# Spreading two weight rows through DRAM and reordering the first group's preparation in a two-layer graph attention kernel

## The chip, the cores and the metric

One core of one Trainium2 chip. The time is the device time of the whole program in microseconds, taken over several runs; one further execution is profiled. Engines are named as the profile names them: PE is TensorE (matrix products and transposes; PEld its weight loads), DVE is VectorE, ACT is ScalarE, POOL is GpSimd, SP is SyncE, which here only issues DMAs. ScalarE issues DMAs too (ACTq).

## The reference

`x` is 64 graphs of 256 nodes with 512 features, `adj` 64 matrices of 256x256 with zeros and ones, all float32. Two layers follow one another:

```python
# layer 0: one head, additive scores
fp = x @ fc_w.T + fc_b
q = fp @ q_w.T + q_b                     # one number for each node
k = fp @ k_w.T + k_b
s = q + k.T + (1 - adj) * -1e9
s = where(s >= 0, s, 0.01 * s)
x = softmax(s) @ fp + x
# layer 1: eight heads, scores with a bias by nodes and log(adj + 1e-9)
Q, K, V = x @ W_q + b_q, x @ W_k + b_k, x @ W_v + b_v
s = Q @ K.T / 8 + (x @ w_g[:512])[:, None] + (x @ w_g[512:])[None, :] + b_g + log(adj + 1e-9)
x = softmax(s) @ V + x
```

In layer 0 the chain x, fp, q can be joined: q is x times one row of 512 numbers, `q_w @ fc_w`, plus a constant, and k likewise.

## The kernel before

The 64 graphs go in 32 groups of two (T = 4 tiles of 128 nodes). A `Group` object has a method for each small step, and `step` writes out by hand, for a window of groups, the order in which the steps of layer 0 of one group, the projections and the attention of layer 1 of another are issued. The schedule is manual: each engine works through its instructions in the order in which the code issues them, and only waits where data or buffers are missing. The products of 512x512 weights are done with seven instead of eight block products (Strassen's scheme in Winograd's form), for which VectorE forms sums of weight blocks once (`blocks_of_weights`, four half-sums of 128x512 for each of wk, wq, wv and fc; the lines L335 to L338) and sums of token blocks for every group.

The change touches only the beginning: the setup and what the first group needs, since it has no older group beside it (`features_first`, in place of the later groups' `mix` and `pf` products). In the order of the code before:

- The weight fc_w is loaded by ScalarE's queue, x, adj (four DMAs), wq, wk, wv and the row wgc_row by SP's queue. `columns` (L249) turns short rows of parameters into columns. `rows_of_x` (L261) multiplies q_w and k_w by fc_w, which gives a 2x512 tile on two partitions (`rows_qk_sb`, copied out of PSUM at L266).
- `spread_rows` (L273, L277) copies each of the two rows to all 128 partitions: a product with a broadcast column of the identity on TensorE into a PSUM bank, and a copy by ScalarE into `wq_row` and `wk_row`. It stands after the first of four tiles of transposes of x (L705), whose results VectorE copies into xT (L706).
- fc_w is transposed (L152; ScalarE copies fcT out, L153). VectorE forms `dot_q` and `dot_k` for the four tiles (L519: multiplies x by the row and sums up), with the constant kqc of k between them (L291).
- `product(t)` (L718) is the feature product of one tile; ScalarE copies it (L722). `queries` (L581) turns q into a row on all partitions by way of TensorE.
- `adjt` (L562) turns adj by 32x32 blocks on VectorE and forms the mask (L564). `weights` (L604, L608 on VectorE, the exponential at L609 on ScalarE) gives layer 0's softmax weights e, `sums` (L658) their sums on TensorE, and `recip_of_sums` (L667, L668) their reciprocals.
- `constants_of_projections` (L301, TensorE, 16 products of 128x256) and its `add` (L313, L317, L318) bring fc_b's part into the biases of layer 1's projections, which lie in the columns `cols_1`.
- In the last loop each tile t of x1 is formed: a product with e (L750), two of the half-sums of wv and fc, then x1 = product * reciprocal + x (L756) on VectorE; then x1 is turned on TensorE (`x1t`, L811, copied by ScalarE at L816).

After that `step` goes on with `pq.p1` (L412), the first block product of layer 1's queries, `pk.p1` and `pv.p1`, the sums of token blocks `xsum` (L375), `keys` (L519, with wgc_row) and the load of the next group's x, which waits for `keys`. Later groups send their q through DRAM to spread it (`spread`, L591 and L593): a write of the 128x4 tile and a broadcast read to 128 partitions.

The PSUM pool `ps` has four banks, taken in turn; one of them holds the constant `pk` until L291 has read it.

Of the kernel before, what the change touches and what calls it, by code (L numbers as in the profile page):

```python
# [10 lines left out]
F32 = mybir.dt.float32  # L11
# [6 lines left out]
P = 128  # L18
# [7 lines left out]
def kernel(  # L26
# [64 lines left out]
    nc = tc.nc  # L91
    NB, N, D = x.shape
# [53 lines left out]
    def transposed_weights(w, pool, psum, copy):  # L146

        t = pool.tile([P, NC, D], F32, tag="fcT", name="fcT")
        for hc in range(NC):
            pt = psum.tile([P, 512], F32, tag="bank", name=f"pfc_{hc}")  # L150
            for oc in range(NC):
                nc.tensor.transpose(pt[:, ts(oc, P)], w[:, oc, ts(hc, P)], ident)  # L152
            copy(t[:, hc, :], pt)  # L153
        return t

    wk_row = const.tile([P, D], F32, tag="wk_row", name="wk_row")
    wq_row = const.tile([P, D], F32, tag="wq_row", name="wq_row")
    kqc = const.tile([P, 1], F32, tag="kqc", name="kqc")

    NR = 4  # L160
# [3 lines left out]
    def fast():  # L164
        main = ExitStack()
        with main:
# [12 lines left out]
            def bank(name):  # L179
                return ps.tile([P, 512], F32, tag="bank", name=name)  # L180
# [87 lines left out]

            def spread_rows(rows):

                for n, dst in enumerate((wq_row, wk_row)):
                    pt = bank(f"row_{n}")
                    nc.tensor.matmul(  # L273
                        pt, lhsT=ident[0:2, n : n + 1].to_broadcast([2, P]), rhs=rows,
                        start=True, stop=True,
                    )
                    nc.scalar.copy(dst, pt)  # L277

            def constant():

# [248 lines left out]
            class Group:  # L529
# [167 lines left out]
                def features_first(self):  # L697

                    g = self.g
                    xT = one.tile([P, NC, TOK], F32, tag="qT", name=f"xT_{g}")  # L700
                    fp = v_all
                    for t in range(T):
                        pt = bank(f"xTp_{g}_{t}")
                        for c in range(NC):
                            nc.tensor.transpose(pt[:, ts(c, P)], self.x[:, t, ts(c, P)], ident)  # L705
                        nc.vector.tensor_copy(  # L706
                            xT[:, :, ts(t, P)], pt.rearrange("p (c n) -> p c n", c=NC)
                        )
                        if t == 0:
                            spread_rows(rows_qk)  # L710
                    fcT = transposed_weights(fc_nat, wts, ps, nc.scalar.copy)
                    for t in range(T):
                        self.dot_q(t)

                    def product(t):
                        pp = bank(f"fp_{g}_{t}")
                        for c in range(NC):
                            nc.tensor.matmul(  # L718
                                pp, lhsT=xT[:, c, ts(t, P)], rhs=fcT[:, c, :],
                                start=(c == 0), stop=(c == NC - 1),  # L720
                            )
                        nc.scalar.copy(fp[:, t, :], pp)  # L722

                    product(0)
                    self.queries()
                    k_constant()
                    for t in range(T):
                        self.dot_k(t)
                    self.adjt(True)
                    product(1)  # L730
                    self.weights(0)
                    self.weights(1)
                    self.add_eps()
                    product(2)
                    add_constants = constants_of_projections()
                    for name, wt in (("k", wk_sb), ("q", wq_sb)):
                        for issue in blocks_of_weights(wt, name):
                            issue()
                    self.sums()
                    columns(rows_1, cols_1, "cols_1")  # L740
                    product(3)
                    add_constants()
                    self.recip_of_sums()
                    self.begin()
                    sums = blocks_of_weights(wv_sb, "v") + blocks_of_weights(fcT, "fc")
                    for t in range(T):
                        gr, ic = divmod(t, TPG)
                        po = bank(f"x1p_{g}_{t}")
                        for j in range(TPG):
                            nc.tensor.matmul(  # L750
                                po, lhsT=self.e0[:, j, gr, ts(ic, P)], rhs=fp[:, gr * TPG + j, :],
                                start=(j == 0), stop=(j == TPG - 1),
                            )
                        for issue in sums[2 * t : 2 * t + 2]:
                            issue()
                        nc.vector.scalar_tensor_tensor(  # L756
                            self.x[:, t, :], po, recip0[:, g, t : t + 1], self.x[:, t, :],
                            ALU.mult, ALU.add,
                        )
                        if t > 0:  # L760
                            self.x1t(t - 1)
                    self.x1t(T - 1)


                def begin(self):
# [341 lines left out]
            def step(d, a, f, n, check):  # L1107


                def of(group):  # L1110
                    def issue(pieces):
                        for piece in pieces.split():
                            name, *args = piece.split(":")
                            if group is None:
                                continue
                            target = group
                            if "." in name:
                                part, name = name.split(".")
                                target = getattr(group, part)
                            getattr(target, name)(*map(int, args))  # L1120
                    return issue

                D, A, F, X = of(d), of(a), of(f), of(n)
                f.older = d
                X("load_adj")
                if a is not None:
                    attention_and_layer_0(D, A, F, X)
                else:
                    f.features_first()
                    F("pq.p1 pq.keep_1 copy:0 pk.p1 pk.keep_1 pv.p1 pv.keep_1")  # L1130
                F("xsum:0 xsum:1 xsum:2 pq.p6")
                A("factor:3:0 factor:3:1 both:3")
                F("keys:2 keys:3 keys:0 keys:1")
                X("load_x")
                F("pq.p7 pq.p2 pq.sum_00 xsum:3")
                check()
                F("pq.p5 pk.p6 pq.sum_11 pq.p3")
                A("divide:0")
                X("dot_q:0 dot_q:1 dot_q:2 dot_q:3 spread")
                F("pq.p4 pq.sum_10 copy:1 copy:2")  # L1140
                A("complete:0 store:0 parts:2")
                if n is None:
                    A("parts:3")
                F("pk.p7 pk.p5 pk.sum_11 residual:0")
                X("adjt")
                F("pk.p2 pk.sum_00")
                X("dot_k:0 dot_k:1")
                F("pk.p3 pk.p4 pk.sum_10")
                X("dot_k:2 dot_k:3")
                F("turn_residual:0")  # L1150
                if n is None:
                    A("attend:1 totals_1 ratios:1 turn:1 divide:1 complete:1 store:1")
                    F("residual:1 turn_residual:1")

                    F("pv.p2 scores:0 pv.p6 pv.sum_00 factor:0:0 factor:0:1 scores:1 both:0 pv.p7")
                    F("factor:1:0 factor:1:1 both:1 scores:2 pv.p5 sums_1:0 scores:3 pv.sum_11")
                    F("ratios_t:0 ratios_r:0 factor:2:0 factor:2:1 pv.p3 pv.p4 factor:3:0 pv.sum_10")
                    F("factor:3:1 attend:0 finish:0 sums_of_e:1 attend:1")
                    F("ratios_t:1 ratios_r:1 finish:1")
                    check_ranges()()  # L1160
                    return
                X("mask add_eps")
                F("pv.p2 pv.p6")
                X("weights:0")
                F("pv.p7 pv.p5")
                X("weights:1")
                F("pv.sum_00")
                A("parts:3")

            with tc.manual_schedule(engines=ENGINES):  # L1170
                f = Group(0)
# [4 lines left out]
                    nc.tensor.matmul(warm[:, 0:P], lhsT=ident, rhs=ident, start=True, stop=True)  # L1176
                columns(rows_0, cols_0, "cols_0")
                rows_qk = rows_of_x()
                k_constant = constant()
                d, a, a_w = None, None, {}  # L1180
                for g in range(NG):
# [224 lines left out]
```

## Time and profile before

| What | Value |
|---|---|
| median of 4 runs | 2311.5 us (2310.65 to 2312.56) |
| profiled execution, its own time | 2312.43 us |
| its span | 2310.6 us |
| mean granted TensorE clock | 0.998 |
| idle time of TensorE in the span | 15.5 us |
| start of the first block product of layer 1 | 45.13 us |
| DMA traffic | 163.84 MB, mean 71 GB/s |
| adj, 128 KB, from issue to landing | 3.6 us (median) |

The span is that of the profiled execution's instructions; its own time is 1.8 us longer. Times inside the profile count from the start of the span. A row of the costliest groups gives line, engine, operation and tiles, and then the busy time, the mean of one instruction and the idle time ahead of it with what ended it. The chain of waits is followed back from the last instruction and says on which engine the time that matters was spent; in its order of time each row is a start, a length on the chain and what ran. A row of the timeline is a start, a length, engine, line, operation and tiles. The granted clock is the share of TensorE's full clock.

### The profile page before, as it was taken

What the parts mean: (1) busy time and instruction counts of PE and PEld (TensorE: products, weight loads), DVE (VectorE), ACT (ScalarE), POOL (GpSimd) and SP (SyncE); (2) the same over time, 40 slices, a digit from 0 to 9 for tenths busy, and PEclk for the clock granted to TensorE, in tenths of its full rate; (3) what the DMA queues carried; (4) which work ended last, traced back from release to release, by engine and by line L of the source; (5) the groups of instructions that cost most, each with busy time, mean ns of one, the idle gap of its engine ahead of it and who ended that gap; (6) DMA issues with size and microseconds to landing.
All of it is one profiled execution on the core that took longest, in us unless ns stands there. A gap on an engine that the chain in (4) does not pass through costs nothing.

```text
span 2310.6 us, 33613 instructions
## 1 busy us (share of the span) xinstructions
PE 2295.1 (99%) x12618; PEld 1902.9 (82%) x12618; DVE 2124.3 (92%) x3180; ACT 1072.2 (46%) x1865; POOL 121.9 (5%) x120
## 2 busy tenths in 40 slices
PE   9999999999999999999999999999999999999997
PEld 5888888888888888888888888888888888888885
DVE  6899999999999999999999999999999999999997
ACT  3544445444445444444444444444544445444443
POOL 0000000000000000000000000000000000000000
PEclk9999999999999999999999999999999999999999
DMA  4122323223323233232233232332223323323312
GB/s 133 42 65 74 78 74 69 65 65 81 84 64 69 60 78 78 74 66 64 69 78 80 63 72 63 81 78 74 61 63 74 78 73 70 64 64 80 84 47 38
DMA packets 517264, 163.84 MB, mean 71 GB/s; under 512 B 415188, under 2 KB 478696, under 8 KB 517096
## 3 DMA queue, kind: packets, MB, share of 16 engines
q1 hardware_dynamic: 514440, 160.32, 29.1%
q8 instruction: 102, 1.67, 0.3%
q10 hardware_dynamic: 2656, 1.31, 0.2%
q14 instruction: 66, 0.54, 0.1%
HBM read 95.43 MB, written 66.12 MB: 70 GB/s over the span
## 4 chain that ended last, share of the span: by engine, by line
PE 98%; DVE 1%; DMA 0%; ACT 0%; issue 0%; ACTq 0%; DVEq 0%
PE pv L412 17%; PE pq L412 17%; PE pf L412 16%; PE pk L412 16%; PE sc L859 11%; PE oT L899 10%; PE y L689 9%; PE fp L718 1%; DMA fc_nat<-in_L_gnn_fc_w_dram 0%; PE rc L637 0%; PE xTp L705 0%; DVE osb L1034 0%; PE tot L927 0%; DVE osb L1040 0%; DVE osb L1033 0%; DVE x L756 0%
## 5 line engine op out<-in xcount | busy, mean ns | idle before, releaser
L873 ACT ACTIVATE e<-sc,c 128x1024 f32<-128x1024 f32 x254 | 269.0, 1110 | 79.1 <-PE sc L859 77.6
L879 DVE TENSOR_TENSOR e<-e,am 128x1024 f32<-128x1024 f32 x254 | 297.8, 1213 | 0.4 <-ACT e L873 0.4
L859 PE MATMUL sc<-qT,kT 64*128 64x256 f32 x2048 | 255.8, 389 | 0.4 <-ACT e L873 0.4
L899 PE MATMUL oT<-e,v 128*64 128x256 f32 x2032 | 233.4, 382 | 0.0
L859 PEld LDWEIGHTS sc<-qT,kT 64*128 64x128 f32 x2048 | 187.2, 186 | 52.8 <-issue 32.8
L495 POOL TENSOR_TENSOR pf_s<-pf_s,x 128x512 f32<-128x512 f32 x93 | 118.4, 1273 | 2107.9 <-ACT pf_s L494 2040.5
L689 PE MATMUL y<-e,x 128*128 128x256 f32 x992 | 225.6, 380 | 0.0
L899 PEld LDWEIGHTS oT<-e,v 128*64 128x64 f32 x2032 | 140.2, 137 | 85.4 <-DVE x L501 10.3
L689 PEld LDWEIGHTS y<-e,x 128*128 128x128 f32 x992 | 186.2, 190 | 24.0
L432 ACT ACTIVATE pq_s<-pq,cols 128x256 f32<-128x256 f32 x192 | 80.5, 470 | 249.1 <-PE pq L412 249.1
L494 ACT ACTIVATE pf_s<-pf,recip 128x256 f32<-128x256 f32 x186 | 77.9, 470 | 197.6 <-PE pf L412 197.6
L917 DVE TENSOR_REDUCE part<-est 128x32 f32<-128x1024 f32 x124 | 151.3, 1220 | 4.3
L916 DVE STREAM_TRANSPOSE est<-es 128x1024 f32<-128x1024 f32 x124 | 152.3, 1229 | 0.0
L886 DVE TENSOR_TENSOR es<-e,e 128x1024 f32<-128x1024 f32 x126 | 149.3, 1206 | 1.1
L695 ACT COPY yT<-y 128x512 f32<-128x512 f32 x124 | 72.6, 585 | 131.6 <-PE y L689 130.9
L429 ACT COPY pk_s<-pk 128x512 f32<-128x512 f32 x96 | 56.3, 586 | 165.7 <-PE pk L412 159.0
L906 ACT COPY oTs<-oT 128x512 f32<-128x512 f32 x128 | 75.0, 586 | 117.3 <-PE oT L899 96.5
L412 PE MATMUL pk<-t1b,wk 128*128 128x256 f32 x512 | 121.1, 379 | 0.4 <-DVE kT L443 0.4
L412 PE MATMUL pv<-wv,t1b_c 128*128 128x256 f32 x512 | 121.1, 379 | 0.0
L412 PE MATMUL pv<-wv,t1b 128*128 128x256 f32 x512 | 121.1, 379 | 0.0
L412 PE MATMUL pq<-x1T,wq 128*128 128x256 f32 x512 | 121.0, 379 | 0.0
L412 PE MATMUL pk<-t1b,k_s 128*128 128x256 f32 x512 | 121.0, 379 | 0.0
(181 smaller groups left out, 4505.9 us busy)
## 6 DMA issues: line engine op xcount, KB each, us to landing
x<-in_x_dram SPq DMA_DIRECT2D x32, 1024.0 KB, 5.1
out_dram<-osb SPq DMA_DIRECT2D x254, 128.0 KB, 3.1
xd<-xt SPq DMA_DIRECT2D x124, 256.0 KB, 2.0
x1T<-xd SPq DMA_DIRECT2D x496, 64.0 KB, 2.0
adj<-in_adj_dram SPq DMA_DIRECT2D x128, 128.0 KB, 3.6
qrow<-q SPq DMA_DIRECT2D x31, 256.0 KB, 4.2
fc_nat<-in_L_gnn_fc_w_dram ACTq DMA_DIRECT2D x4, 256.0 KB, 4.9
wq<-in_L_gnn_W_q_dram SPq DMA_DIRECT2D x1, 1024.0 KB
```

Source lines behind the costliest of these rows:

```text
L412: nc.tensor.matmul(o, lhsT=lk[:, ts(m, P)] if len(lk.shape) == 2 else lk[:, m], rhs=rk, start=(start and m == 0 and k == 0), stop=(m == 1 ...
L432: nc.scalar.activation(dst[:, m], src[:, m], AF.Identity, bias=self.bias[:, 2 * o + m : 2 * o + m + 1],)
L494: nc.scalar.mul(s[:, m], src[:, m], self.recip[:, TPG * k + m : TPG * k + m + 1])
L495: nc.gpsimd.tensor_tensor(s, s, self.out(o, k), ALU.add)
L689: nc.tensor.matmul(y[:, ts(gr, N)], lhsT=self.x[:, gr * TPG + j, ts(c, P)], rhs=self.e0[:, j, gr, :], start=(gr == 0 and j == 0), stop=(gr ...
L859: nc.tensor.matmul(sc[:, par, pr, :], lhsT=self.kT[rows, 2 * hg + pr, ts(t, P)], rhs=self.qT[rows, 2 * hg + pr, ts(gr, N)], start=True, st ...
L873: nc.scalar.activation(e, sc, AF.Exp, bias=self.c[:, t : t + 1], scale=SCALE)
L879: nc.vector.tensor_tensor(ef, ef, self.am[:, jc, u // 2, :].unsqueeze(1).to_broadcast([P, 4, N]), ALU.mult,)
L886: nc.vector.tensor_tensor(self.esum[u], self.e[u, 0], self.e[u, 1], ALU.add)
L899: nc.tensor.matmul(oT[par * HD : (par + 1) * HD, pr, :], lhsT=self.v[:, gr * TPG + jc, ts(h, HD)], rhs=self.e[2 * gr + hg, jc][:, par, pr, :],
L916: nc.vector.transpose(turned, self.esum[u].rearrange("p a b i -> p (a b i)"))
L917: nc.vector.tensor_reduce(self.part[:, hg, :], turned.rearrange("p (m c) -> p m c", c=B), AX.X, ALU.add,)
```

## The change

- `spread_rows` no longer uses TensorE and PSUM. ScalarE issues a DMA that writes the 2x512 tile to DRAM (4 KB), waits for it, and issues a second DMA that reads the 1024 numbers back to each of the 128 partitions of one tile `qk_rows` (512 KB). It is called right after `rows_of_x` and `constant`, before the transposes of x.
- `adjt(True)` moves from behind `dot_k` to before `dot_q` on VectorE.
- The four feature products stand nearly in a row: `queries` comes between the second and the third, and the fourth now precedes `sums`.
- k's half-sums come directly behind `weights`; `constants_of_projections` and `columns` go behind `sums`, `recip_of_sums` behind the first x1 product, the addition of the constants behind the second. q's and v's half-sums stand in the loop over t (before: v's and fc's).
- fc's half-sums are issued in `step`, after `xsum` 0 to 2 and `pq.p6`.
- `add_eps` (ScalarE) moves behind the constants.

```diff
--- before.py
+++ after.py
@@ -153,8 +153,8 @@
             copy(t[:, hc, :], pt)
         return t
 
-    wk_row = const.tile([P, D], F32, tag="wk_row", name="wk_row")
-    wq_row = const.tile([P, D], F32, tag="wq_row", name="wq_row")
+    qk_rows = const.tile([P, 2, D], F32, tag="qk_rows", name="qk_rows")
+    wq_row, wk_row = qk_rows[:, 0], qk_rows[:, 1]
     kqc = const.tile([P, 1], F32, tag="kqc", name="kqc")
 
     NR = 4
@@ -268,13 +268,11 @@
 
             def spread_rows(rows):
 
-                for n, dst in enumerate((wq_row, wk_row)):
-                    pt = bank(f"row_{n}")
-                    nc.tensor.matmul(
-                        pt, lhsT=ident[0:2, n : n + 1].to_broadcast([2, P]), rhs=rows,
-                        start=True, stop=True,
-                    )
-                    nc.scalar.copy(dst, pt)
+                d = dram.tile([2 * D], F32, tag="qk", name="qk_rows_d")
+                nc.scalar.dma_start(d.rearrange("(n h) -> n h", n=2), rows)
+                nc.scalar.dma_start(
+                    qk_rows.rearrange("p n h -> p (n h)"), d.unsqueeze(0).to_broadcast([P, 2 * D])
+                )
 
             def constant():
 
@@ -706,9 +704,8 @@
                         nc.vector.tensor_copy(
                             xT[:, :, ts(t, P)], pt.rearrange("p (c n) -> p c n", c=NC)
                         )
-                        if t == 0:
-                            spread_rows(rows_qk)
                     fcT = transposed_weights(fc_nat, wts, ps, nc.scalar.copy)
+                    self.adjt(True)
                     for t in range(T):
                         self.dot_q(t)
 
@@ -722,27 +719,23 @@
                         nc.scalar.copy(fp[:, t, :], pp)
 
                     product(0)
-                    self.queries()
                     k_constant()
                     for t in range(T):
                         self.dot_k(t)
-                    self.adjt(True)
                     product(1)
+                    self.queries()
+                    product(2)
                     self.weights(0)
                     self.weights(1)
+                    for issue in blocks_of_weights(wk_sb, "k"):
+                        issue()
+                    product(3)
+                    self.sums()
+                    add_constants = constants_of_projections()
+                    columns(rows_1, cols_1, "cols_1")
                     self.add_eps()
-                    product(2)
-                    add_constants = constants_of_projections()
-                    for name, wt in (("k", wk_sb), ("q", wq_sb)):
-                        for issue in blocks_of_weights(wt, name):
-                            issue()
-                    self.sums()
-                    columns(rows_1, cols_1, "cols_1")
-                    product(3)
-                    add_constants()
-                    self.recip_of_sums()
                     self.begin()
-                    sums = blocks_of_weights(wv_sb, "v") + blocks_of_weights(fcT, "fc")
+                    sums = blocks_of_weights(wq_sb, "q") + blocks_of_weights(wv_sb, "v")
                     for t in range(T):
                         gr, ic = divmod(t, TPG)
                         po = bank(f"x1p_{g}_{t}")
@@ -751,6 +744,10 @@
                                 po, lhsT=self.e0[:, j, gr, ts(ic, P)], rhs=fp[:, gr * TPG + j, :],
                                 start=(j == 0), stop=(j == TPG - 1),
                             )
+                        if t == 0:
+                            self.recip_of_sums()
+                        if t == 1:
+                            add_constants()
                         for issue in sums[2 * t : 2 * t + 2]:
                             issue()
                         nc.vector.scalar_tensor_tensor(
@@ -760,6 +757,7 @@
                         if t > 0:
                             self.x1t(t - 1)
                     self.x1t(T - 1)
+                    self.later = blocks_of_weights(fcT, "fc")
 
 
                 def begin(self):
@@ -1129,6 +1127,9 @@
                     f.features_first()
                     F("pq.p1 pq.keep_1 copy:0 pk.p1 pk.keep_1 pv.p1 pv.keep_1")
                 F("xsum:0 xsum:1 xsum:2 pq.p6")
+                if a is None:
+                    for issue in f.later:
+                        issue()
                 A("factor:3:0 factor:3:1 both:3")
                 F("keys:2 keys:3 keys:0 keys:1")
                 X("load_x")
@@ -1176,6 +1177,7 @@
                     nc.tensor.matmul(warm[:, 0:P], lhsT=ident, rhs=ident, start=True, stop=True)
                 columns(rows_0, cols_0, "cols_0")
                 rows_qk = rows_of_x()
+                spread_rows(rows_qk)
                 k_constant = constant()
                 d, a, a_w = None, None, {}
                 for g in range(NG):
```

## The prediction

> **What bounds the kernel now.** I read first the totals of the page and the shares of its chain of waits, then the busy time of each engine in two stretches (0 to 11 us is the first load), then the chain in order of time for the start, and last VectorE's timeline there.
>
> ```profile
> PE 2295.1 (99%) x12618; PEld 1902.9 (82%) x12618; DVE 2124.3 (92%) x3180; ACT 1072.2 (46%) x1865; POOL 121.9 (5%) x120
> PE 98%; DVE 1%; DMA 0%; ACT 0%; issue 0%; ACTq 0%; DVEq 0%
> ```
> ```profile
> 11.00:45.30 34.30, 33.68 (x158) 18.86 (x158) 28.19 (x56) 11.90 (x23) 0.00 (x0) 0.95 0.48 131
> ```
> ```profile
> 45.30:2300.00 2254.70, 2252.79 (x12438) 1880.33 (x12437) 2091.57 (x3109) 1058.80 (x1841) 118.38 (x93) 1.00 0.29 69
> ```
>
> The columns after the stretch are its length, the busy time of PE, PEld, DVE, ACT and POOL, the granted clock, the DMA share and GB/s. From 45.3 us on TensorE stands still for 1.9 us in 2254.7. The diff takes nothing from TensorE there; it touches the first group's preparation, which ends when `pq.p1`, the first product of layer 1, starts. So the sum is one number: how far that start moves. Every later product follows it one for one, as long as nothing that the change pushes behind it becomes late.
>
> ```profile
> 11.80 1.91 PE row L273 x4
> 13.71 2.50 PE xTp L705 x12
> ...
> 18.83 3.43 PE fp L718 x8
> 22.26 0.44 PE qrow L581 x4
> 22.70 6.87 PE fp L718 x16
> 29.57 1.86 PE pc L301 x32
> 31.43 0.44 PE sm L658 x16
> ...
> 32.02 3.63 PE fp L718 x8
> ...
> 35.91 0.37 DVE cols L317 x4
> ...
> 36.46 0.09 DVE recip L668
> ...
> 43.82 0.71 DVE x L756
> ...
> 45.29 1.73 PE pq L412 x8
> ```
>
> The reader should see two stretches. Up to 35.9 us the chain lies on TensorE, almost without a gap. From 36.46 us it lies on VectorE: the reciprocals, then eight half-sums of weights of 0.6 to 0.7 us and four rows of x1 of 0.7 us with no idle time, until the last x1 at 43.82 us; 1.47 us later `pq.p1` starts. What counts is when the reciprocals start, and what VectorE has to do behind them.
>
> ```profile
> 16.85 0.68 DVE L519 CUSTOM_DVE_ANT_0 jq<-x,wq_row 128x512 f32<-128x512 f32 x1
> 23.08 1.24 DVE L562 STREAM_TRANSPOSE am<-adj 128x1024 f32<-128x1024 f32 x1
> ```
> ```profile
> qrow<-q SPq DMA_DIRECT2D x31, 256.0 KB, 4.2
> ```
>
> The dots with the rows of q and k begin at 16.85 us, and adj is turned after them.
>
> **TensorE up to the sums.** Taken out are the two products that spread the rows (1.91 us on the chain at 11.80) and two ScalarE copies (0.58 and 0.59 us, beside other work). Without them the first feature product starts at 18.83 - 1.91 = 16.9 us; the copies of xT on VectorE (0.69 us each) and the copies of fcT on ScalarE can hold it to about 18. The four products now come ahead of the sums: 3.43 + 3.44 + 0.44 (queries) + 3.43 + 3.63 = 14.4 us. TensorE could thus start the sums of e (`sm`) at 16.9 + 14.4 = 31.3 us.
>
> **The rows by way of DRAM.** The rows are in SBUF at 11.37 us (ScalarE's copy, 10.80 + 0.57). The nearest row is the same trip that each later group makes for q: its first transfer was issued at 61.81 us and the second at 63.28 us, 1.47 us later, and the second, 256 KB, lands 4.2 us after its issue. Here the second is 512 KB. The traffic of the 256 KB was spread over 2.1 us (six slices of 0.35 us), so I add 2.1 us: 11.4 + 1.5 + 6.3 = 19.2 us with the engines free. They aren't: from 13 to 25 us the DMA share is 0.94 to 1.09 in every microsecond, first with adj (small packets, about 160 GB/s), then with three weights of 1 MB. Sharing with them I estimate at 2 us more: 21.2 us. The bound above is the row of `wgc_row`, 256 KB broadcast too, which took 10.0 us behind those weights: 11.4 + 1.9 + 10.0 = 23.3 us. The bound below is 19.2 us.
>
> The Trainium skill's page "DMA: Bandwidth & Descriptors", section "Anatomy of one DMA", speaks against such a trip: each DMA pays about 2 us whatever its size, most of it the receipt of the last write, heaviest where DRAM is written. The trace has 1.47 us for the small write to DRAM, less than the page. By the page the two would take 2.0 and 2.0 + 512 KB at 436 GB/s = 3.2 us and be there at 16.6 us; the rows would then not decide and the sum would be that with adj alone, below.
>
> ScalarE waits for the first transfer with the copies of fcT behind it. The fcT transposes that feed them begin at 13.5 us at the earliest (11.80 + 1.7 for the remaining transposes at the speed of the first four), so the wait, over by 12.9 us to 13.5 us, hides in front of them. If it lasted to 16 us, the first product would lose its 1.9 us again.
>
> **Adj first.** The turning of adj and the mask take 2.1 us (23.08 to 25.16) and now precede the dots. The last adj transfer is issued at about 13.6 us and lands 3.8 us later, at 17.4 us; before, 5 us of dots covered this, now VectorE waits for it from 14.7 us (four copies of 0.72 us from 11.84). So the dots cannot start before 17.4 + 2.1 = 19.5 us. With the broadcast taking a share of the same 16 engines I put the landing 1.3 us later: 20.8 us. The dots start at J = the later of the two, 21.2 us, between 19.5 and 23.3.
>
> From the dots to the sums VectorE's rows are: dots 16.85 to 23.16 = 6.3 us, weights 25.16 to 29.05 = 3.9 us, last exponential 0.67 us; together 10.9 us. The queries on TensorE need only the first half of the dots (J + 2.9 = 24.1 us, against 16.9 + 6.9 = 23.8 us). The sums start at 21.2 + 10.9 = 32.1 us, 0.8 us behind what TensorE could.
>
> **Constants behind the sums.** From the sums to the reciprocals there are now 0.44 (sm) + 1.86 (pc) + 0.15 (columns) + 1.8 (first x1 product, a quarter of 7.2 us) + 0.3 (turn of the sums and start) = 4.55 us: 32.1 + 4.55 = 36.65 us, against 36.46. The half-sums of k are done before that (J + 10.2 + 2.9 = 34.3 us), and VectorE idles about 2 us there. Behind the reciprocals stand again eight half-sums (q and v in place of v and fc) and four x1, and in addition the constants of the columns, 0.37 + 0.16 = 0.53 us, which before lay ahead. So `pq.p1` moves by 36.65 - 36.46 + 0.53 = +0.7 us: the 1.9 us that TensorE saves are used up, because VectorE both starts the dots 4 us later and carries as much work behind the reciprocals as before.
>
> **Behind `pq.p1`.** The four half-sums of fc (2.8 us) go in front of `keys`. VectorE idles 5.1 us there before it adds qT at 55.76 us, which hides them. The load of the next x waits for `keys`: it moves from 50.71 to 53.5 us and lands 5.1 us later at 58.6 us; the dots that read it begin at 58.90 us. If that cover failed by 1 us, the next addition (62.60 us, 0.8 us of idle time ahead of it) would slip by 0.2 us. fc itself is wanted only by group 1's feature product. On SP's queue nothing is moved; adj of group 1, which waits for the turning, is issued some 3 us earlier, behind the weights. I cost all this at nothing.
>
> **The sum.** The profiled execution took 2312.43 us with a span of 2310.6 us. With +0.7 us it would take 2313.1; the median of the four runs lies 0.9 us below the profiled one, so 2311.5 + 0.7 = 2312.2 us.
>
> **The rivals.** A difference of 0.2% is 4.6 us; that is about what a measurement of this kernel can tell from no change.
>
> First: the saving passes through. If the transfers hardly disturb each other, J = 19.5 us, the sums start where TensorE allows, at 31.3 us at the latest, and the move is 31.3 + 4.55 - 36.46 + 0.53 = -0.1 us. If also the dip of the clock (granted 0.50 from 14 to 17 us, 0.82 in the next microsecond, a loss of 1.7 us) doesn't recur, J alone holds: 30.4 + 4.55 - 36.46 + 0.53 = -1.0 us, 2310.5. For it: adj has landed by 17.4 us in the trace. Against it: the saturated engines. It cannot give 4.6 us, since the 1.9 us of products and 1.7 us of clock are all there is to gain.
>
> Second, the other side: the broadcast is starved on the way to the dots. Each microsecond of J beyond 20.4 us goes to the end undiminished, as VectorE has no slack between the dots and the sums. At 23.3 us the move is +2.8 us, 2314.3. From J = 25.1 us it is over 4.6 us; if the rows had to wait until the weights' traffic ends at 25.3 us, with a microsecond for the landing, the move is +5.8 us, 2317.3. For it: `wgc_row`'s 10 us, and that both transfers stand in the fullest stretch of the trace. Against it: fc_w on ScalarE's queue and x on SP's shared the same engines at the start, both 1 MB, and finished within 1.3 us of each other, so a second queue isn't left behind.
>
> **How the numbers follow.** The forecast (-0.5 to +2 us) gets 0.63, the saving passing through 0.15, the rows late but under 4.6 us 0.10, the rows late by more 0.09; what I have not seen, 0.03. The scatter of the four runs is about 1 us to each side of the median. The range goes from the first rival's -1.0 us less 1.1 (2309.4) to the bound of `wgc_row`, +2.8 us and 1.1 (2315.4), and leaves out the starved case. Faster by over 0.2%: 0.03; slower: 0.11; within: 0.86.
>
> **What would show it.** In the profile after, the dots (jq) start near 21 us with an idle spell of some 6 us before the turning of adj, ended by a DMA; the first feature product starts near 17 us; `sm` follows the exponential, not the fourth product; the reciprocals stand near 36.7 us, with v's and q's sums and the constants behind them and no idle time; `pq.p1` starts at 46.0 us. I am wrong if the rows land after 25 us, if ScalarE's copies of fcT wait past 16 us, or if TensorE stands still after `pq.p1`.

## The result, and the profile after

| | before | after |
|---|---|---|
| median | 2311.24 us (60 runs, 2309.58 to 2312.93) | 2314.82 us (40 runs, 2313.23 to 2316.64) |
| profiled execution | 2312.43 us, span 2310.6 us | 2314.62 us, span 2312.8 us |

The ratio is 1.0015 (95% interval 1.0011 to 1.0019): the change makes the kernel 3.6 us slower (2.5 to 4.4). That is within 0.2% and inside the range, but the sum had +0.7 us. The profiled pair differs by 2.2 us.

The totals of the page and the two stretches first, with the columns as before:

```profile
PE 2293.2 (99%) x12614; PEld 1899.6 (82%) x12614; DVE 2124.1 (92%) x3180; ACT 1071.9 (46%) x1863; POOL 122.0 (5%) x120
```
```profile
11.00:45.30 34.30, 31.37 (x154) 16.10 (x153) 25.29 (x52) 10.56 (x21) 0.00 (x0) 1.00 0.55 146
45.30:2300.00 2254.70, 2252.93 (x12438) 1879.52 (x12436) 2094.05 (x3113) 1059.44 (x1841) 118.41 (x93) 1.00 0.29 69
```

The long stretch is what it was: TensorE stands still for 1.8 us in it (1.9 before), in the same 12438 instructions. In the short one TensorE has 2.3 us less work, and the clock is 1.00 where it was 0.95. Of the chain of waits after, in order of time (start, length, what ran), these pieces carry the start:

```profile
12.87 5.96 DMA adj<-in_adj_dram
18.85 1.26 DVE am L560
20.73 0.68 DVE jq L517
30.79 0.64 ACT e L607
31.47 0.43 PE sm L656 x8
33.78 1.91 PE x1p L743 x4
35.84 0.18 DVE recip L666
45.19 1.73 PE pq L410 x8
```

From 11 us on the chain no longer lies on TensorE: it waits for the load of adj, goes to VectorE, and stays there up to the exponential at 30.79 us. `pq.p1` starts at 45.19 us, 0.1 us *earlier* than before (45.29). In this pair the 2.2 us are therefore not in the first group, and not in the steady part either. The last work instruction of both kernels, VectorE's cast of the final flag, and the engine queues' waits at the end show where they are (timeline of before, then of after; then SyncE's waits from 2303 us, in us, count, longest, of before and of after):

```profile
2304.47 0.14 DVE L1101 CAST flag<-oks 1x1 int32<-1x1 f32 x1
```
```profile
2304.61 0.14 DVE L1099 CAST flag<-oks 1x1 int32<-1x1 f32 x1
```
```profile
SPq L1401 <- PEq L1401: 0.6, 2, 0.4
```
```profile
SPq L1403 <- PEq L1403: 2.6, 2, 2.4
```

The casts end 0.13 us apart. From there to the end of the span it is 5.96 us before and 8.09 us after. In this tail nothing of the result is computed: every engine reads the flag, branches past the general version of the program that the kernel keeps for other inputs, drains and meets the rest. The rows of the program's closing line (L1401, L1403) show who is late (duration in ns as least, median, most, then first and last start; before, then after):

```profile
L1401 DVEq DRAIN  x2: 10/14/17, 2309.7 to 2310.1; - x2
```
```profile
L1403 ACTq DRAIN  x2: 8/8/8, 2306.4 to 2310.4; - x2
L1403 DVEq DRAIN  x2: 17/73/129, 2310.0 to 2312.5; - x2
```

ScalarE reaches its last drain at 2310.4 us, VectorE at 2312.5 us; before, both were there at 2310.1. So the profiled pair puts nearly the whole difference (2.1 of 2.2 us) at the end of the program, 2260 us behind the change.

### The profile page after: what moved, and what is told of

Same layout as the page of the kernel before. It is cut to its first block, busy times and chain, and to the rows that moved or that the text cites. A ratio compares the mean times of both kernels' runs of the same rounds, so it can differ in the third digit from the quotient of the medians.

```text
span 2312.8 us, 33603 instructions
## 1 busy us (share of the span) xinstructions
PE 2293.2 (99%) x12614; PEld 1899.6 (82%) x12614; DVE 2124.1 (92%) x3180; ACT 1071.9 (46%) x1863; POOL 122.0 (5%) x120
## 4 chain that ended last, share of the span: by engine, by line
PE 97%; DVE 2%; DMA 1%; ACT 0%; SPq 0%; issue 0%; DVEq 0%
PE pv L410 17%; PE pq L410 17%; PE pf L410 16%; PE pk L410 16%; PE sc L857 11%; PE oT L897 10%; PE y L687 9%; DMA x<-in_x_dram 0%; DMA adj<-in_adj_dram 0%; PE rc L635 0%; DVE jk L517 0%; DVE osb L1032 0%; PE tot L925 0%; DVE osb L1038 0%; DVE osb L1031 0%
```

## The experiments

Two things had to be told apart: what the change does to the first group, and what the tail does. Two figures serve as measure in every run. The *preparation* is the start of `pq.p1` minus the start of the first transposition of x (`xTp`), both from the timeline; counted like this, the arrival of x, which puts that transposition anywhere from 9.85 to 11.46 us, drops out. The *tail* is the time from the end of the flag's cast to the end of the span. With 11 runs of a variant, an interval is about 0.09% to each side, 2 us; what is smaller rests on rows of the profiles. "Records" counts everything that VectorE executed in the trace, its waits for semaphores included.

| Kernel | median, us | ratio (95%) | preparation, us | VectorE records | tail, us |
|---|---|---|---|---|---|
| before (profiled) | 2311.24 | 1 | 33.96 (clock dip) | 3725 | 5.96 |
| before_again | 2311.67 (one) | | 33.76 (clock dip) | 3725 | 5.94 |
| before_less | 2313.57 | 1.0011 (1.0002 to 1.0020) | 32.66 | 3720 | 8.28 |
| before_pad8 | 2312.13 | 1.0004 (0.9995 to 1.0013) | 32.64 | 3733 | 6.68 |
| after (profiled) | 2314.82 | 1.0015 (1.0011 to 1.0019) | 34.25 | 3721 | 8.09 |
| after_again | 2315.08 (one) | | 34.34 | 3721 | 8.11 |
| after_pad8 | 2313.49 | 1.0008 (0.9999 to 1.0018) | 34.74 | 3729 | 6.51 |
| rows_by_te | 2315.12 | 1.0016 (1.0007 to 1.0025) | 34.22 | 3721 | 7.77 |
| dots_first | 2314.82 | 1.0016 (1.0007 to 1.0025) | 32.92 | 3723 | 8.74 |
| reorder_only_pad8 | 2313.57 | 1.0006 (0.9997 to 1.0015) | 34.21 | 3731 | 6.55 |
| dram_alone_pad8 | 2313.46 | 1.0005 (0.9996 to 1.0014) | 36.34 (clock dip) | 3733 | 6.85 |
| dots_first_pad8 | 2313.24 | 1.0007 (0.9998 to 1.0016) | 39.32 (clock dip) | 3731 | 6.53 |
| dots_first_q_pad8 | 2312.71 | 1.0004 (0.9995 to 1.0014) | 33.02 | 3731 | 6.63 |
| rows_on_sp | 2310.57 | 0.9996 (0.9987 to 1.0005) | 31.51 | 3730 | 6.78 |

The kernel before stood at 2311.51, 2311.49 and 2311.28 us beside the three sets of runs.

The two measures carry nearly everything. The stretch between them, from the start of `pq.p1` to the end of the cast, is 2259.5 to 2260.1 us in all profiles but that of dots_first_q_pad8 (2260.9). Preparation plus tail, less the 38.6 us of a before without the dip of the clock (32.65 + 5.95), gives the difference of each variant's median to the before beside it to within 0.7 us. The exceptions are dram_alone_pad8 and dots_first_pad8, where the profiled execution was the slowest of its set.

**after_pad8: eight idle instructions more on VectorE.** The theory for the tail: what counts is how many instructions VectorE executes. The change takes none of its work (3180 busy instructions in both profiles), but four of its semaphore waits.

```diff
+    extra = const.tile([P, 8], F32, tag="extra", name="extra")
+    for n in range(8):
+        nc.vector.memset(extra[:, n : n + 1], 0.0)
```

> The changed kernel with eight tiny VectorE instructions (128x1 memsets of a tile that nobody reads) ahead of everything, in VectorE's idle first 5 us. Theory: 2.1 us of the loss lie behind the work, where VectorE's last instruction waits for instruction loading because the change shortened VectorE's stream by four instructions. Then the end of the work (the flag's cast) stays where it is in the changed kernel, the tail from there to the end of the span falls from 8.1 to 6.0 us, and the time is 2314.8 - 2.1 = 2312.7 us. Rival, the whole loss lies in the first 45 us and the tail's 2 us are chance: 2314.8 us.

Measured: 2313.49 us, 1.3 us below after where 2.1 was expected, and the tail is back to 6.51 us (8.09). More instructions and less time: the tail's cost is not one of work. The preparation of this profile is half a microsecond longer (34.74 us), because here the rows land last, at 20.15 us: VectorE waits 2.96 us for them with adj already turned. The last wait of SyncE is as short as before:

```profile
SPq L1406 <- PEq L1406: 0.6, 2, 0.4
```

**before_less: fewer instructions in the kernel before.** The same theory from the other side. The edit leaves out the first of the range checks of the softmax reciprocals, that of groups 0 to 3, and touches nothing of the change.

```diff
-    if d is not None and (d.g % NR == NR - 1 or d.g == NG - NR // 2 - 1):
+    if d is not None and d.g > NR and (d.g % NR == NR - 1 or d.g == NG - NR // 2 - 1):
```

> The kernel before without the first of its range checks of the reciprocals (groups 0 to 3): at least five VectorE instructions fewer, and nothing else. Theory: VectorE's stream is then as short as in the changed kernel, its last instructions fall on the far side of the same boundary, the tail grows from 6.0 to 8.1 us and the time from 2311.2 to 2313.3 us although the kernel does less; if six fewer step past the boundary again, 2311.2 us. Rival, instruction places don't matter: 2311.2 us or a little less, tail 6.0 us.

Measured: 2313.57 us; with less work the old kernel is 2.1 us slower. VectorE executes five records fewer, and its very last one, a semaphore instruction, comes at 2311.9 us, where TensorE's is at 2310.3 (closing line, columns as above):

```profile
L1401 DVEq EVENT_SEMAPHORE  x2: 21/21/21, 2309.7 to 2311.9; - x2
```

**rows_by_te: the new order, but the rows spread by TensorE again.** It asks whether the trip through DRAM matters at all.

```diff
-                d = dram.tile([2 * D], F32, tag="qk", name="qk_rows_d")
-                ...
+                for n, dst in enumerate((wq_row, wk_row)):
+                    pt = bank(f"row_{n}")
+                    nc.tensor.matmul(
+                    ...
+                    nc.scalar.copy(dst, pt)
...
+                        if t == 0:
+                            spread_rows(rows_qk)
...
-                spread_rows(rows_qk)
```

> The changed kernel with the rows spread by TensorE as before; everything else of the change is kept. Theory, adj's landing holds the dots, not the rows: the first feature product moves 1.9 us later, adj lands some 0.7 to 1.3 us earlier for want of the broadcast (dots at 19.4 to 20.0 us in place of 20.7), the sums follow TensorE at about 31.3 us, and the first product of layer 1 starts within 0.5 us of the changed kernel's 45.0 us: 2314.8 us, or 2312.7 us if the tail is short. Rival, the trip through DRAM is what costs (the step of the prediction): the dots move 2 us or more and the time falls by over 1 us beyond the tail. Second rival, the trip brings its full 1.9 us: 1.9 us slower than the changed kernel.

Measured: 2315.12 us against 2314.82, preparation 34.22 against 34.25 us. The two products and copies that the change takes out, 1.91 us of TensorE on the old chain, are worth nothing in the new order, but not because the same wait decides in both. Here the chain lies on TensorE, as the expectation said of the sums, and VectorE waits for the row of `queries` (chain of waits, then VectorE's timeline):

```profile
17.70 6.87 PE fp L719 x16
24.57 0.44 PE qrow L581 x4
25.01 6.87 PE fp L719 x16
31.87 0.57 PE sm L658 x16
```
```profile
26.21 1.27 DVE L604 SCALAR_TENSOR_TENSOR e<-qrow,kq,e 128x256 f32<-128x256 f32 x2 [0.70 <-ACT qrow L586]
```

VectorE waits only 0.90 us for adj (4.93 in after) and begins the dots at 19.20 us, 7.8 us after the first transposition, where after takes 10.0 us. The last transfer of adj takes 3.7 us from issue to landing here and 6.0 us in after, beside the broadcast. So what the trip through DRAM saves on TensorE, it loses by holding up adj.

**dots_first: after with adj turned behind the dots again.**

```diff
                     fcT = transposed_weights(fc_nat, wts, ps, nc.scalar.copy)
-                    self.adjt(True)
                     for t in range(T):
                         self.dot_q(t)
...
                     for t in range(T):
                         self.dot_k(t)
+                    self.adjt(True)
                     product(1)
```

> The changed kernel with adj turned behind the dots again; everything else of the change is kept. Theory: the rows are there at about 16.2 us, so the dots start at 16.3 us in place of 20.7, the turning hides behind them, the sums start at about 29.5 us and layer 1's first product 1.9 us earlier than in the changed kernel, at about 43.1 us: 2312.9 us with a tail of 8 us, 2310.8 us with one of 6 us. Rival, the rows through DRAM come too late by themselves: the dots wait for them past 19 us and the gain is under 0.5 us.

In the profile it is right: the dots start at 16.93 us, the preparation is 32.92 us, 1.3 us shorter than in after. But the median stays at 2314.82 us, because the tail is 8.74 us (3723 records), and because the runs scatter over 5 us (2313.5 to 2318.4): the dots now depend on the arrival of the rows alone, which is the likely reason (the profiled execution is the fastest of them). The tail had to be taken out of the comparison, so the next kernels carry the eight instructions too.

**reorder_only_pad8: both undone, only the moved products, sums and constants left** (the edits of rows_by_te, dots_first and after_pad8 together).

> The changed order of products, constants and half-sums alone: the rows are spread by TensorE and adj is turned behind the dots, both as before, and eight tiny VectorE instructions at the start keep the end of the program clear of the boundary (tail about 6 us). Theory: the order itself costs. The first feature product starts at about 17.4 us, four products lead to sums at 31.8 us, 4.55 us more to the reciprocals, and behind them stand eight half-sums and the constants: layer 1's first product at 45.6 us, where the kernel before without a dip of the clock has 43.7 us. Time 2311.3 + 1.9 = 2313.2 us. Rival, the order is harmless and only adj ahead of the dots costs: 43.7 us and 2311.3 us.

Measured: `pq.p1` at 45.45 us, preparation 34.21 us, against 32.64 us in before_pad8. The new order costs 1.6 us by itself. Here it is TensorE again: with its two products of rows it begins the feature products at 17.41 us, `queries` now stands behind two of them in place of one (24.28 us, in before_pad8 21.07), VectorE waits for it, and the sums come behind the fourth product at 31.68 us (30.22). From VectorE's timeline:

```profile
26.07 1.26 DVE L607 SCALAR_TENSOR_TENSOR e<-qrow,kq,e 128x256 f32<-128x256 f32 x2 [1.66 <-ACT qrow L589]
```

**dram_alone_pad8: the kernel before, with the rows by way of DRAM and nothing else of the change** (the new `spread_rows`, called ahead of `constant` as in after, and the eight instructions).

> The kernel before with the rows sent through DRAM, nothing else changed but the eight tiny VectorE instructions. Theory: TensorE saves its 1.9 us but the sums of e wait for the exponentials, whose dots start no earlier than before (rows at 16.2 us or later); layer 1's first product stays within 0.5 us of 43.7 us and the time within 0.7 us of 2311.3 us. Rival, the saving passes through: 2309.4 us.

Measured: 2313.46 us, between 2311.48 and 2315.71, and so slower than expected. The profiled execution is the slowest of them: VectorE waits 5.66 us for the rows and begins the dots at 19.79 us, and the clock dips at 23.21 us. In that execution the saving does not pass through in the old order either, because the rows come late; the other runs were not profiled.

**dots_first_pad8** is dots_first with the eight instructions.

> The changed kernel with adj turned behind the dots, with eight tiny VectorE instructions at the start. Theory: the work is as in the run without them (flag at about 2303 us, first product of layer 1 at 43.3 us), and the tail falls from 8.7 to about 6.2 us: 2314.8 - 2.5 = 2312.3 us by the median. Rival, the scatter of that run had another cause than the tail: no change from 2314.8 us.

The tail came down as expected (6.53 us). The median, 2313.24 us, is 1 us above the expectation, and the profiled execution (2318.23 us) shows why the runs spread up to there: its rows landed at 21.8 us, and VectorE stood still for 8.1 us.

```profile
21.97 0.69 DVE L520 CUSTOM_DVE_ANT_0 jq<-x,qk_rows 128x512 f32<-128x512 f32 x1 [8.13 <-DMA qk_rows<-qk_rows_d]
```

**dots_first_q_pad8** is dots_first_pad8 with q's half-sums formed while VectorE waits for the sums, in place of behind the reciprocals.

```diff
                     sums = blocks_of_weights(wq_sb, "q") + blocks_of_weights(wv_sb, "v")
+                    for issue in sums[:4]:
+                        issue()
+                    sums = [lambda: None] * 2 + sums[4:] + [lambda: None] * 2
```

> The same with q's four half-sums issued ahead of the reciprocals, into VectorE's idle time, so that only v's four stand behind them (two between the second and third x1, two before the fourth... one pair ahead of x1 of tile 1 and one ahead of tile 2). Theory: behind the reciprocals VectorE then has 2.8 us less to do, the reciprocals come about 0.4 us later, TensorE becomes the limit and layer 1's first product starts at 42.6 to 43.0 us: 0.4 to 0.8 us less than with the half-sums of q behind. Rival, VectorE was not what held the x1 tiles: no change.

Measured: 2312.71 us, 0.5 us less. The profiled execution began its dots at 17.95 us, when the rows had landed, and `pq.p1` at 43.53 us, later than the 42.6 to 43.0 us expected; its preparation is 33.02 us. The step is within the noise of the runs.

**rows_on_sp: the same kernel, but SyncE issues the two DMAs of the rows, ahead of adj, the weights and wgc_row.** If the scatter of the rows comes from the transfers they share the DMA engines with, this takes it away.

```diff
-            adj_0 = load_adj(0)
...
-            wq_sb = weights(W_q, "wq", wts)
-            ...
-            wgc_row = row(w_g[D : 2 * D], "wgc_row")
...
-                nc.scalar.dma_start(d.rearrange("(n h) -> n h", n=2), rows)
-                nc.scalar.dma_start(
+                nc.sync.dma_start(d.rearrange("(n h) -> n h", n=2), rows)
+                nc.sync.dma_start(
...
                 spread_rows(rows_qk)
...
+                f.a = load_adj(0)
+                wq_sb = weights(W_q, "wq", wts)
+                ...
+                wgc_row = row(w_g[D : 2 * D], "wgc_row")
```

> The last variant (adj turned behind the dots, q's half-sums ahead of the reciprocals, eight tiny VectorE instructions) with the trip of the rows issued on SP's queue and adj and the weights issued behind it, so that nothing of size runs beside the broadcast. Theory, it is the company of adj and the weights that makes the rows late and scattered: the rows land about 3.8 us after the second issue, at 16.2 to 16.8 us, in every run; the dots start then, the sums near 29.8 us, layer 1's first product at 42.6 to 43.0 us; adj lands near 20 us, in time for its turning at 22.4. Median 2310.4 us, 0.9 us under the kernel before, with a spread of the runs as small as its own. Rival, the trip scatters by itself: the dots start between 17 and 22 us again and the median stays at 2312.7 us.

Measured: 2310.57 us, between 2309.14 and 2311.19. Timeline of SyncE and VectorE:

```profile
11.03 0.25 SPq L270 DMA_DIRECT2D qk_rows_d<-rows_qk_sb  x1
12.25 0.32 SPq L271 DMA_DIRECT2D qk_rows<-qk_rows_d  x1
...
16.48 0.69 DVE L515 CUSTOM_DVE_ANT_0 jq<-x,qk_rows 128x512 f32<-128x512 f32 x1 [2.53 <-DMA qk_rows<-qk_rows_d]
```

The 512 KB are there 4 us after their issue, adj at 19.7 us, in time for its turning at 22.6 us behind the dots. The preparation is 31.51 us, 1.1 us shorter than in before_pad8, and the runs lie as close together as those of before. It is 4.2 us below after, and 0.7 us below before, which its interval doesn't tell from no change; beside before_pad8, which carries the same eight instructions, it is 1.6 us less. The edit changes the queue and the order of the loads at once, and which of the two makes the rows punctual is not told apart.

**before_pad8** prices the eight instructions themselves.

> A control: the kernel before with the eight tiny VectorE instructions alone. Theory: they run in VectorE's idle first 5 us and move its stream further from the boundary: tail 6.0 to 6.6 us, median within 0.6 us of 2311.4 us. Rival, the eight instructions themselves cost, and the other variants that carry them are to be read as that much faster: over 1 us slower.

Measured: 2312.13 us beside 2311.28, ratio 1.0004 (0.9995 to 1.0013); the tail is 6.68 us where it was 5.95. That is more than the 0.6 us and the 6.6 us expected, but the interval doesn't tell the median from no change. All seven padded kernels have a tail of 6.5 to 6.9 us, so each may be read some 0.6 to 0.9 us lower; whether the instructions themselves cost this is not shown. The run also brings the preparation of the old order without a dip of the clock, 32.64 us.

**after_again and before_again** are both kernels unaltered, a second profile of each.

> The changed kernel, unaltered, for a second profile. Theory: tail again about 8.1 us; the dots start between 19.5 and 22 us, held by adj or by the rows, whichever lands last this time, and layer 1's first product moves with them. Rival, the 18.85 us landing of adj is fixed: dots at 20.7 us again to within 0.2 us.

> The kernel before, unaltered, for a second profile. Theory: tail about 6 us; without a dip of the clock between 14 and 17 us, layer 1's first product starts at about 43.7 us in place of 45.1, so that the changed kernel's start at 45.0 us is 1.3 us later, like for like. Rival, 45.1 us is the rule: 45 us again.

The tails repeat: 8.11 and 5.94 us. In after_again adj landed at 19.46 us, was turned from 19.48 us, and the dots began at 21.37 us, so adj is what holds them. The expectation for before missed: it had the dip again (from 13.37 us), and yet `pq.p1` at 43.86 us, since x had come a microsecond sooner. That is why the table counts from the first transposition.

## Why the prediction was right or wrong, step by step

**Right: where the limit goes.** Two readings of before's profile held, that with the rows off TensorE VectorE sets the reciprocals once adj is turned ahead of the dots, and that it carries as much behind them as ever. In the timeline of after the idle spell and the shorter one at the reciprocals stand where they were put (6 and 2 us were named):

```profile
18.85 1.25 DVE L560 STREAM_TRANSPOSE am<-adj 128x1024 f32<-128x1024 f32 x1 [4.93 <-DMA adj<-in_adj_dram]
...
35.84 0.18 DVE L666 RECIPROCAL recip<-rc 128x4 f32<-128x4 f32 x1 [1.86 <-PE rc L665]
```

The dots start at 20.73 us (forecast 21.2), the sums' second half at 31.47 (32.1), released by the exponential and not by the fourth product, as said, though only 0.24 us behind it. From there to the reciprocals it is 4.37 us (4.55), and `pq.p1` is at 45.19 us (46.0). The first feature product starts at 14.90 us, where 16.9 to 18 was forecast: besides the 1.91 us, the clock did not dip. Little came of that, for `queries` and the sums waited for VectorE. Behind `pq.p1` the half-sums of fc are hidden, as costed: VectorE works at them from 47.64 to 50.5 us and still idles 2.34 us before it adds qT at 55.66 us (55.76 before).

**Right by luck: the rows.** The term for the broadcast was too large: landing at 21.2 us forecast, bounds 19.2 to 23.3, and 17.0 us in the profile of after. The dots hardly moved by it, since they waited for adj, which the forecast had at 18.7 us (dots at 20.8 us by adj alone) and which landed at 18.8 us. The forecast came to that figure from 17.4 us for adj in before, where the trace has 17.07, and from too small a price for the broadcast beside it: 1.3 us, where the last transfer of adj took 2.1 us longer than in before (5.95 and 3.81). The Trainium skill's page "DMA: Bandwidth & Descriptors", section "Anatomy of one DMA", gives a fixed 2 us and 436 GB/s, fitted on DMAs that GpSimd issues; an estimate by these two has the rows at 16.6 us, and this one execution agrees with it better than with my bounds. The runs as a whole don't: from its issue the same 512 KB took 4.6 us in after, 7.6 us in after_pad8 and 7.9 us in dots_first_pad8. The page's 3.2 us for this size, an estimate too, is nearest to the 4.0 us of rows_on_sp, where the broadcast goes ahead of the loads; no run has it alone. Rival 2 named this mechanism, and it does occur: in after_pad8 the rows decide, in after and after_again adj does.

**Wrong: "The sum".** That step took the +0.7 us against the profiled execution and then went down 0.9 us to the median. Two things are missing in it.

First, the clock. The profiled execution of before had the dip of the clock that rival 1 spoke of; the same 3.41 us from 13.95 us on, in before and in before_pad8 (columns as above):

```profile
13.95:17.36 3.41, 3.41 (x19) 3.41 (x17) 2.50 (x4) 0.64 (x2) 0.00 (x0) 0.50 1.01 168
```
```profile
13.95:17.36 3.41, 3.33 (x27) 2.77 (x27) 2.70 (x6) 1.75 (x3) 0.00 (x0) 1.00 1.02 149
```

With the dip the old preparation takes 33.96 and 33.76 us (before, before_again), without it 32.66 and 32.64 us (before_less, before_pad8): it costs before 1.2 us, as its chain lies on TensorE there. None of the profiles of after, after_again, after_pad8 and rows_by_te had it (their clock is 1.00 from 9 to 45.3 us), and in after, where a load and VectorE set the pace up to the sums, its absence can bring little (no profile of after has one to compare). So a part of the 0.9 us between the profiled run and the median was probably this dip, and it is no constant that may be carried over to the changed kernel. Against an undisturbed before, the change costs 34.25 - 32.65 = 1.6 us in the preparation, not 0.7. The rival that the saving passes through fell too: it needed the dots at 19.5 us and they began at 20.73, and what it wanted to gain from the clock is gained by before as well, in those executions that have no dip.

Second, the end of the program. No part of the prediction looked there, since the diff touches only the start. The tail is 8.09 - 5.96 = 2.1 us longer.

Together 1.6 + 2.1 = 3.7 us against a before without the dip. How often the executions behind the median have it isn't settled; if all had it, 1.2 us would go off. The sum is 2.5 to 3.7 us, and 3.6 us were measured (2.5 to 4.4).

**Where the 1.6 us come from.** The new order asks two things to be early, and after gives only one of them. With rows by TensorE (reorder_only_pad8 and rows_by_te) TensorE reaches `queries` and the sums too late, wherever adj is turned; with the rows through DRAM and adj turned first (after) VectorE begins the dots too late. Each is enough for 34.2 us, and that the two come out alike is chance. With both out of the way the preparation is 32.92 us (dots_first), and 31.51 us where q's half-sums, too, have left the path behind the reciprocals and the rows come at 16.3 us (rows_on_sp).

**What stays open.** What VectorE waits for at the end is inferred. Shown is that the tail goes with that total: the five profiles with fewer than 3725 records (3720, 3721 three times, 3723) have VectorE's last records late and a tail of 7.8 to 8.7 us; the nine with 3725 or more have 5.9 to 6.9 us, whatever they compute. In before_less one record is late, in after, after_again and rows_by_te the last two, in dots_first the last four: in each case those past the 3719th, the first of which follows its predecessor by 2.1 to 3.0 us. The branch past the general version tells the two groups apart as well. It is VectorE's record 3715, 3716 or 3718 in the five and 3720 or later in the nine, so only in the five does the limit fall among the few records behind it. Every profile has 3.7 to 4.4 us between that branch and VectorE's next record, whatever the tail; in before:

```profile
L1368 DVEq COMPARE_BRANCH  x1: 72/72/72, 2305.7 to 2305.7; - x1
L1368 DVEq EVENT_SEMAPHORE  x1: 21/21/21, 2309.6 to 2309.6; - x1
```

Between 2308 and 2313 us the DMA queues of after carry three transfers of instructions and nothing else (queue, kind: packets, MB, share of the 16 engines):

```profile
q8 instruction: 1, 0.02, 1.7%
q14 instruction: 2, 0.02, 1.2%
```

They start near 2310.4 us, and VectorE's late drain follows at 2312.5 us. In before such transfers come at 2310.2 us as well, and VectorE's records go on without such a gap. The Trainium skill's page "Runtime: NRT & Kernel Launch", section "Instruction fetch mechanics", says that an engine's instructions are fetched in blocks of 16 KB, 256 instructions, by DMA while it executes, and that crossing a block is mostly hidden. A limit at a fixed count fits that, and then the crossing is not hidden here: it costs 2.1 us. A limit that lies ahead of the branch would cost nothing of its own, if the wait behind the branch covers it; that fits the nine, but neither this nor the fetch was tried by itself.

## What to carry to other kernels

Before changing an order, ask which engine's wait ends last in the stretch: the 1.9 us of TensorE that this change saves are worth nothing where VectorE waits for a load, and the same trip through DRAM gives a preparation a microsecond shorter than the old one once it is issued ahead of the loads that crowd it, adj is turned behind the dots and q's half-sums are out of the way. A transfer put beside others has its price there: here the broadcast held up the very load that VectorE waits for. For differences of a few microseconds compare the head, the steady part and the tail of two profiles each by itself, and count the head from the arrival of its input; a shift in the head can be outweighed by one at the very end that comes only from the number of instructions. A profiled execution's distance to the median belongs to that kernel alone, and is not an offset for the next one.

## What the runs showed of the hardware that was not expected

- The end of the program can cost 2.1 us more when an engine executes a few instructions fewer: a VectorE total of 3725 records gives a tail of 5.96 us, one of 3720 gives 8.28 us, and eight idle instructions more take after's 8.09 us to 6.51 us.
- A broadcast of 512 KB from DRAM took 4.6 to 7.9 us from issue to landing when it shared the DMA engines with another queue's loads, and 4.0 us when it was issued ahead of them. The last 128 KB of adj took 6.0 us beside it (after) and 3.7 us without it (rows_by_te).
- The clock's dip to 0.50 lasted 3.41 us each time, and came at 13.95, 13.37 or 23.21 us, at 34.93 us in dots_first_pad8, or not at all (ten of the fourteen profiles have none between 9 and 2299 us); before loses 1.2 us by it.
